# Moving small start-up DMAs from SyncE to GpSimd, and widening the dummy matmuls of the start, in a three-layer CIN kernel

## The chip, the cores and the metric

The kernel runs on one core of a Trainium2 chip. A core has five engines that run their own instruction streams and meet at semaphores: TensorE (PE in the profile; its weight loads are PEld), VectorE (DVE), ScalarE (ACT), GpSimd (POOL) and SyncE (SP). SP, ACT and POOL can issue DMAs. The metric is the device time of one execution in microseconds, as the median of several runs: 736.74 us before the change (three runs, 736.66 to 737.49).

## The reference

A batch of 1024 samples has 39 fields with an embedding of 64 each. Three layers of a compressed interaction network (CIN) follow, all in float32:

```python
def _cin_layer(Xk, X0, W, b):
    O = W.shape[0]
    Hk, Fdim = (Xk.shape[1], X0.shape[1])
    Wr = W.reshape(O, Hk, Fdim)
    return jnp.einsum('bhe,bfe,ohf->boe', Xk, X0, Wr) + b[None, :, None]
X0 = sparse_embedding
Xk = X0
outs = []
for W, b in ((W0, b0), (W1, b1), (W2, b2)):
    Xk = _cin_layer(Xk, X0, W, b)
    outs.append(Xk.sum(axis=-1))
cin_output = jnp.concatenate(outs, axis=-1)
return cin_output @ fc_w.T + fc_b
```

Every layer has 64 outputs. Only sums over the embedding reach the result, one number per sample, through a final linear layer. The biases b0, b1, b2 and fc_b are vectors of 64 words (fc_b: one word).

## The kernel before, in words

The two later layers are folded into the weights first: from W2 and the final weights the kernel makes a small matrix V2 (`v2`, 64 x 40), from W1 and V2 the products `pt` and `pv` (L431), and together with W0, transposed into `pw` (L452), these fill one table `both` of 128 x (39 x 40). What is left for the samples is a sum over pairs of fields, products of two rows of x. Weights for the pairs are taken from `both` into `pairs` (L480 and L482), turned by TensorE (`tr`, L499) and copied to `wa` (L500 and L501).

The samples are done in 32 blocks of 2048 columns (32 samples times 64). For each block GpSimd gathers five tiles of 128 rows, each row one field's values, from a table `xd` in DRAM (`roll`, through L170); every second block it also gathers two smaller tiles `u` and `v` (`roll_small`). VectorE multiplies two gathered tiles into a product `p` (L210; L212 for u and v), and TensorE multiplies `p` by `wa` into PSUM banks `po` (L515, and L535 and L546 for u and v). Six products per block and one joint product per two blocks follow each other as steps; VectorE works four steps ahead of TensorE (`AHEAD`). When a block is through, `finish` reads its banks with ScalarE (L563) and VectorE (L565, which adds the bias `b0s`) and sums them up (L576).

The table `xd` has three DRAM tiles, each for two blocks: 39 rows of fields and a row of ones for each block. `load(n)` writes a block's fields (L164). Block 0 is treated apart: it is loaded in two halves `xh` (L244), gathered straight from there, and copied into `xd` by SP afterwards (L387).

The order of the work on each engine is the order of the program text (a manual schedule); a semaphore is waited for where a buffer is written or read by another engine or a DMA. DMAs of a kind share eight semaphore lanes in turn, so a DMA also waits until the one that used its lane before has landed. In the start-up the queues hold, in order:

- SP: `fcrow`, the first half `xh`, three DMAs of `ones` into `xd` (L253), two for `w0s` (L255), two for `bias` (L357: b1 and b2), two for `b0s` (L359), one for `fcb` (L360), the two copies `xd<-xh` (L387).
- ACT: `w2s`, two halves of `w1s`, the second half `xh`.
- POOL: small set-up work (its last memset is L355), four gathers from the first half `xh`, `load(1)`, four from the second half, tile 4 of block 0, u and v, the five gathers of block 1, `load(2)`, `load(3)`, and then the gathers of block 2.

TensorE's own start is filled with dummy matmuls on constants into a bank `idle` (`spin`, L273). A dummy has 256 columns unless another width is given; each matmul in float32 stands in the profile as two records. There are two at the very start, then after the small matmuls of `fcrow` one of 256 and one of 128, again one of 256 and one of 128 after the four matmuls of `pv` (L397), three behind V2, and one more ahead of the first L515.

Of the kernel before, what the change touches and what calls it, by code (L numbers as in the profile page):

```python
# [60 lines left out]
B, F, E, H = 1024, 39, 64, 64  # L61
FH = F * H
FT = F + 1
# [12 lines left out]
MM = 512  # L76
# [7 lines left out]
NTAB = 3  # L84
# [59 lines left out]
def cin_kernel(ctx: ExitStack, tc: tile.TileContext, x, w0t, b0, w1, b1, w2, b2, fc_w, fc_b, out):  # L144
    nc = tc.nc
# [10 lines left out]
    xd = [dram.tile([2 * FT, BLK], F32, name=f"xd{k}") for k in range(NTAB)]  # L156
# [5 lines left out]
    def load(n, engine=nc.sync):  # L162
        first = n % 2 * FT
        engine.dma_start(  # L164
            xd[n // 2 % NTAB][first : first + F].rearrange("f (b e) -> f b e", e=E),
            xv[:, n * BB : (n + 1) * BB, :],
        )

    def gather_rows(dst, table, k):
        nc.gpsimd.indirect_dma_start(  # L170
            dst, None, table, bass.IndirectOffsetOnAxis(ap=lists[:, k : k + 1], axis=0)
        )

    def roll(n, tiles=range(NT)):
        for i in tiles:
            k = n % 2 * NT + i
            gather_rows(rt[n % 2][:, i], xd[n // 2 % NTAB][: FT if k < NT else 2 * FT], k)

    def roll_small(n):
        table = xd[n // 2 % NTAB].rearrange("f (t c) -> (f t) c", c=SUB)  # L180
        for k, dst in enumerate((ut, vt)):
            gather_rows(dst[n // 2 % 2], table, 2 * NT + k)
# [5 lines left out]
    bias = const.tile([H, 2], F32, name="bias")  # L188
    b0s = const.tile([128, 1], F32, name="b0s")
    fc0s = const.tile([128, 1], F32, name="fc0s")  # L190
    fcb = const.tile([1, 1], F32, name="fcb")
# [24 lines left out]
    with prep as prep:  # L216
# [6 lines left out]
        ones = prep.tile([16, 2, 128], F32, name="ones")  # L223
# [25 lines left out]
        for s in range(2):  # L249
            half = slice(s * FH // 2, (s + 1) * FH // 2)  # L250
            nc.scalar.dma_start(w1s[:, half], w1[:, half])
        for k in range(NTAB):
            nc.sync.dma_start(xd[k][F::FT].rearrange("r (p c) -> p r c", c=128), ones)  # L253
        for s, n in enumerate((NW, F - NW)):
            nc.sync.dma_start(  # L255
                w0s[H * s : H * s + F, 0 : n * H], w0v[:, s * NW * H : (s * NW + n) * H]
# [14 lines left out]
        def spin(n=1, cols=MM // 2):  # L271
            for _ in range(n):
                nc.tensor.matmul(  # L273
                    idle[:, 0:cols],
                    nc.const_aps.tensor(1.0, (128, 128), F32),
                    nc.const_aps.tensor(1.0, (128, cols), F32),
                    start=True,
                    stop=True,
                )

        spin(2)

        tmp = prep.tile([128, 16], F32, name="tmp")
        wide = prep.tile([128, 5, NT], F32, name="wide")
# [3 lines left out]
        def new():  # L288
            used[0] += 1
            return tmp[:, used[0] - 1 : used[0]]  # L290
# [24 lines left out]
        for at, k, h in ((1, 0, 0), (2, 1, 0), (3, 2, 0), (4, 0, H)):  # L315
# [4 lines left out]
                start=True,  # L320
                stop=True,
            )
        spin()
        spin(1, MM // 4)

        nc.vector.tensor_copy(row, place)
        step(row, F, 1.0, j)
# [25 lines left out]
        nc.gpsimd.memset(pairs[:, NPAIR:, 0:SQUARE], 0.0)  # L353
        bothv = both.rearrange("p (a b) -> p a b", b=FT)
        nc.gpsimd.memset(bothv[0:H, :, F], 0.0)  # L355
        for k, t in enumerate((b1, b2)):
            nc.sync.dma_start(bias[:, k : k + 1], t.rearrange("(h o) -> h o", o=1))  # L357
        for h in (0, H):
            nc.sync.dma_start(b0s[h : h + H], b0.rearrange("(h o) -> h o", o=1))  # L359
        nc.sync.dma_start(fcb, fc_b.rearrange("(p o) -> p o", o=1))  # L360

        r, most, seat, far = (new() for _ in range(4))
        both_of = prep.tile([128, 2], F32, name="both_of")
# [41 lines left out]
            blocks.rearrange("p f h -> p (f h)").rearrange("p (f h) -> p f h", h=32),  # L405
            pv[:, 0:320].rearrange("p (h f) -> p f h", f=10),
        )
        spin()
        spin(1, MM // 4)
        nc.scalar.copy(v2[:, F:FT], small[0:H, 2:3])  # L410
        for u, f0 in enumerate(quarters):
            for s in range(2):
# [5 lines left out]

        roll_small(0)
        roll(1)  # L420
        load(2, nc.gpsimd)
        load(3, nc.gpsimd)

# [15 lines left out]
        def copy_t(q):  # L439
            for t in range(2):  # L440
                a = 2 * NQ * q + t
                m = len(range(a, min(F, 2 * NQ * (q + 1)), 2))
                copies[t](  # L443
                    bothv[H:128, a : a + 2 * m - 1 : 2],
                    pt[q][H * t : H * t + H, 0 : m * FT].rearrange("h (a b) -> h a b", b=FT),
                )
# [17 lines left out]
                copies[k](bothv[0:H, a + t : a + t + 2 * m - 1 : 2, 0:F], src[:, :, 0:F])  # L464
        copy_t(2)
        copy_t(3)
        spin(3)
        first = [prods.tile([128, BLK], F32, name="p", tag="p") for _ in range(4)]


# [140 lines left out]
    p = {}  # L611
# [25 lines left out]
    for at, (n, c) in enumerate(steps[:-TAIL]):  # L637
# [26 lines left out]
        if at + AHEAD < len(steps):  # L664
            n, c = steps[at + AHEAD]
# [70 lines left out]
```

## Time and profile before

| what | us |
|---|---|
| median of the runs | 736.74 |
| the profiled execution's own time | 743.94 |
| its span, first to last instruction | 742.2 |
| PE busy | 731.6 (99%) |
| DVE busy | 637.7 (86%) |
| POOL busy | 378.7 (51%) |
| ACT busy | 165.4 (22%) |
| L515, main products on PE | 666.9, 1536 records |
| L210, products on DVE | 434.2, 198 instructions |
| L170, gathers of `r` from `xd` on POOL | 306.4, 156 instructions |
| dummies, L273 | 9.1, 20 records |

The profile is one execution; times in its views count from the start of its span. A busy row says how long an engine had an instruction in work, not that it worked at its best; matmuls are pipelined and their ends are modelled. In the timelines, a bracket behind a row tells how long the engine had been idle before it and what released it; "issue" means that nothing in the profile explains the wait. Rows of SPq are DMAs being issued: their lengths are the time to issue, not to land. A row of POOL with a DMA is the time in which GpSimd makes its descriptors.

### The profile page before, as it was taken

To read this page: it belongs to the slowest core of one execution; us is meant where nothing else is said; L and a number is where in the kernel's file an instruction comes from. 1 tells how busy PE (TensorE), PEld (TensorE's weight loads), DVE (VectorE), ACT (ScalarE), POOL (GpSimd) and SP (SyncE) were. 2 spreads that over 40 slices of the span, in tenths; PEclk is the share of its full clock that TensorE was granted. 3 is DMA by queue.
4 is the path that set the end of the run, shared out by engine and by line. 5 is a ranking of instruction groups with operands and counts; after the bars stand their busy time and mean duration, and the time that the engine had idled before them with its cause. 6 is when DMAs were issued, how large, how long until landed. Compare 5 with 4: busy or idle time off the path is not lost.

```text
span 742.2 us, 6521 instructions
## 1 busy us (share of the span) xinstructions
PE 731.6 (99%) x2460; PEld 322.0 (43%) x2460; DVE 637.7 (86%) x518; ACT 165.4 (22%) x241; POOL 378.7 (51%) x248
## 2 busy tenths in 40 slices
PE   8799999999999999999999999999999999999998
PEld 6344444444444444444444444444444444444443
DVE  4798898888998888898888989888898888899885
ACT  2222122221222212122221222212122221212222
POOL 5867453755444575454656545475553557545300
PEclk9999999999999999999999999999999999999999
DMA  8989777867578785767967677786858866666700
GB/s 244 416 262 399 269 280 283 331 225 279 229 291 334 267 302 220 287 239 301 352 216 274 256 278 296 283 312 221 288 232 296 341 264 250 219 249 263 283 1 1
DMA packets 63866, 197.25 MB, mean 266 GB/s; under 512 B 37846, under 2 KB 37943, under 8 KB 43866
## 3 DMA queue, kind: packets, MB, share of 16 engines
q0 software_dynamic: 28784, 186.17, 64.7%
q1 hardware_dynamic: 34104, 9.23, 5.4%
q10 hardware_dynamic: 946, 1.44, 0.7%
q8 instruction: 19, 0.31, 0.2%
q14 instruction: 13, 0.11, 0.0%
HBM read 196.76 MB, written 10.60 MB: 279 GB/s over the span
## 4 chain that ended last, share of the span: by engine, by line
PE 98%; DVE 1%; issue 0%; another core or an unknown queue 0%; ACT 0%; POOL 0%
PE po L515 90%; PE po L535 4%; PE po L546 2%; PE idle L273 1%; PE pt L431 1%; PE pv L431 0%; PE pw L452 0%; PE tr L499 0%; PE pv L397 0%; DVE g L565 0%; DVE sums L587 0%; ACT z L563 0%; POOL shifts L308 0%; DVE wide L295 0%
## 5 line engine op out<-in xcount | busy, mean ns | idle before, releaser
L515 PE MATMUL po<-p,wa 128*128 128x512 f32 x1536 | 666.9, 595 | 0.0
L210 DVE TENSOR_TENSOR p<-r 128x2048 f32<-128x2048 f32 (+2 forms) x198 | 434.2, 2224 | 74.6 <-PE po L515 74.6
L170 POOL DMA_INDIRECT r<-xd,lists x156 | 306.4, 1964 | 297.6 <-issue 283.8
L515 PEld LDWEIGHTS po<-p,wa 128*128 128x128 f32 x1536 | 290.8, 191 | 371.3 <-issue 352.6
L563 ACT ACTIVATE z<-po,fc0s 64x512 f32<-64x512 f32 x128 | 87.3, 682 | 382.5 <-PE po L546 219.7
L565 DVE SCALAR_TENSOR_TENSOR g<-po,b0s,z 64x512 f32<-64x512 f32 x128 | 95.9, 749 | 9.3 <-ACT z L563 5.3
L558 ACT COPY g<-r 39x1024 f32<-39x1024 f32 x64 | 66.7, 1043 | 151.9 <-DVE sums L576 124.7
L576 DVE TENSOR_REDUCE sums<-g 103x16 f32<-103x1024 f32 x62 | 75.6, 1220 | 2.1
L535 PE MATMUL po<-p,wa 32*64 32x512 f32 x512 | 31.6, 600 | 0.0
L170 POOL DMA_INDIRECT u<-xd,lists x16 | 28.3, 1771 | 5.2 <-issue 5.2
L170 POOL DMA_INDIRECT v<-xd,lists x16 | 28.4, 1777 | 4.9 <-issue 4.9
L212 DVE TENSOR_TENSOR p<-u,v 128x1024 f32<-128x1024 f32 x16 | 19.5, 1218 | 0.0
L535 PEld LDWEIGHTS po<-p,wa 32*64 32x64 f32 x512 | 9.4, 131 | 20.2 <-issue 20.2
L546 PE MATMUL po<-u,wa 32*64 32x512 f32 x256 | 17.0, 587 | 0.0
L170 POOL DMA_INDIRECT r<-xh,lists x8 | 7.8, 973 | 6.8 <-DVE blocks L404 4.6
L273 PE MATMUL idle<-const-float32-1.0 128*128 128x256 f32 (+1 forms) x20 | 9.1, 610 | 1.0 <-PEq L723 0.8
L546 PEld LDWEIGHTS po<-u,wa 32*64 32x64 f32 x256 | 5.8, 132 | 8.0 <-issue 8.0
L443 DVE COPY both<-pt 64x200 f32<-64x200 f32 x3 | 1.1, 358 | 7.7 <-remote 5.2
L273 PEld LDWEIGHTS idle<-const-float32-1.0 128*128 128x128 f32 x20 | 6.0, 324 | 2.8 <-issue 1.8
L499 PE MATMUL tr<-unit,pairs 128*128 128x128 f32 x8 | 2.6, 320 | 4.4 <-remote 3.9
L482 DVE TENSOR_TENSOR pairs<-both 128x2 f32<-128x2 f32 (+27 forms) x59 | 6.0, 171 | 0.4 <-ACT both L443 0.4
L500 ACT COPY wa<-tr 128x128 f32<-128x128 f32 x8 | 2.1, 265 | 16.9 <-PE tr L499 15.9
(88 smaller groups left out, 55.4 us busy)
## 6 DMA issues: line engine op xcount, KB each, us to landing
xd<-in_x SPq DMA_DIRECT2D x26, 312.0 KB
r<-xd,lists POOLq DMA_INDIRECT x156
xd<-in_x POOLq DMA_DIRECT2D x5, 312.0 KB
w2s<-in_w ACTq DMA_DIRECT2D x1, 624.0 KB
w1s<-in_w ACTq DMA_DIRECT2D x2, 312.0 KB
xd<-xh SPq DMA_DIRECT2D x2, 156.0 KB
u<-xd,lists POOLq DMA_INDIRECT x16
v<-xd,lists POOLq DMA_INDIRECT x16
```

The lines of the kernel that those rows point to most:

```text
L170: nc.gpsimd.indirect_dma_start(dst, None, table, bass.IndirectOffsetOnAxis(ap=lists[:, k : k + 1], axis=0))
L210: nc.vector.tensor_tensor(p[:, cols], r[:, i, cols], r[:, k, cols], ALU.mult)
L212: nc.vector.tensor_tensor(p[:, 0:SUB], ut[n // 2 % 2], vt[n // 2 % 2], ALU.mult)
L273: nc.tensor.matmul(idle[:, 0:cols], nc.const_aps.tensor(1.0, (128, 128), F32), nc.const_aps.tensor(1.0, (128, cols), F32), start=True, sto ...
L431: nc.tensor.matmul(pt[q][H * t : H * t + H, g * FT : g * FT + FT], w1v[:, a], v2, start=True, stop=True,)
L515: nc.tensor.matmul(po[n][m], wa[:, c, side : side + 2 * H], p[:, bass.ts(m, MM)], start=n % 2 == 0 and c == 0, stop=n % 2 == 1 and c == NP ...
L535: nc.tensor.matmul(dst[half * H : half * H + H], wa[rows, NPAIR, at : at + H], p[rows, bass.ts(side, MM)], start=t >= 2, stop=t < 2 and ha ...
L546: nc.tensor.matmul(dst[half : half + H], wa[rows, NPAIR + 1, H : 2 * H], ut[n // 2 % 2][rows, bass.ts(side, MM)], start=False, stop=t < 2,)
L558: nc.scalar.copy(gt[H : H + F], rt[n % 2][0:F, 0, bass.ts(m, SUB)])
L563: nc.scalar.activation(z[one], po[n][m][other], AF.Identity, bias=fc0s[other])
L565: return lambda: nc.vector.scalar_tensor_tensor(g[n][m // 2][0:H, at], po[n][m][one], b0s[one], z[one], ALU.add, ALU.mult)
L576: nc.vector.tensor_reduce(sums[:, b_at : b_at + SB], g[n][m // 2].rearrange("p (b e) -> p b e", e=E), AX.X, ALU.add,)
```

## The change

The three DMAs of `ones` go from SP to POOL, where they stand ahead of the first gather. The five DMAs of the biases (`bias` twice, `b0s` twice, `fcb`) go from SP to POOL behind the gathers of block 1 and ahead of `load(2)` and `load(3)`. The first two dummies of 256 columns become one of 512; the two places with 256 and 128 columns get one of 512 each; the three of 256 behind V2 become one of 512 and one of 256. The dummy ahead of the first L515 stays. Lines behind the change move up by one to seven.

```diff
-        for k in range(NTAB):
-            nc.sync.dma_start(xd[k][F::FT].rearrange("r (p c) -> p r c", c=128), ones)
         for s, n in enumerate((NW, F - NW)):
             nc.sync.dma_start(
                 w0s[H * s : H * s + F, 0 : n * H], w0v[:, s * NW * H : (s * NW + n) * H]
...
-        spin(2)
+        spin(1, MM)
...
-        spin()
-        spin(1, MM // 4)
+        spin(1, MM)
...
         bothv = both.rearrange("p (a b) -> p a b", b=FT)
         nc.gpsimd.memset(bothv[0:H, :, F], 0.0)
-        for k, t in enumerate((b1, b2)):
-            nc.sync.dma_start(bias[:, k : k + 1], t.rearrange("(h o) -> h o", o=1))
-        for h in (0, H):
-            nc.sync.dma_start(b0s[h : h + H], b0.rearrange("(h o) -> h o", o=1))
-        nc.sync.dma_start(fcb, fc_b.rearrange("(p o) -> p o", o=1))
+        for k in range(NTAB):
+            nc.gpsimd.dma_start(xd[k][F::FT].rearrange("r (p c) -> p r c", c=128), ones)
...
-        spin()
-        spin(1, MM // 4)
+        spin(1, MM)
         nc.scalar.copy(v2[:, F:FT], small[0:H, 2:3])
...
         roll_small(0)
         roll(1)
+        for k, t in enumerate((b1, b2)):
+            nc.gpsimd.dma_start(bias[:, k : k + 1], t.rearrange("(h o) -> h o", o=1))
+        for h in (0, H):
+            nc.gpsimd.dma_start(b0s[h : h + H], b0.rearrange("(h o) -> h o", o=1))
+        nc.gpsimd.dma_start(fcb, fc_b.rearrange("(p o) -> p o", o=1))
         load(2, nc.gpsimd)
         load(3, nc.gpsimd)
...
         copy_t(3)
-        spin(3)
+        spin(1, MM)
+        spin()
```

## The prediction

> **What bounds the kernel.** I read the page first. Its chain that ended last says almost the whole span is TensorE:
>
> ```profile
> PE 98%; DVE 1%; issue 0%; another core or an unknown queue 0%; ACT 0%; POOL 0%
> ```
>
> L515, the main products, is 90% of it and runs with no gap from about 33 us to the end. The change touches nothing behind block 2, so it can act only through the moment at which L515 starts, the pace of its first matmuls, or a starved block soon after. So the second view is the same chain in order of time, for the first 60 us:
>
> ```profile
> 5.96 1.28 PE pv L397 x8
> 7.24 1.58 PE idle L273 x4
> ...
> 8.92 2.63 PE pt L431 x40
> ...
> 18.50 2.72 PE idle L273 x6
> 21.21 3.12 another core or an unknown queue
> ...
> 25.12 0.45 PE tr L499
> ```
>
> (Start, length, what.) L431 is the V2 stage: W1 times V2 into `pt` and `pv`, with W0's transposes (L452) between. It begins at 8.92, when ScalarE has copied `v2`; the first transpose for the main loop runs at 25.12. The chain ends V2 at 18.26 and then has 3 us of nobody. The third view, VectorE's timeline, shows what really paces it:
>
> ```profile
> 11.09 0.36 DVE L443 COPY both<-pt 64x200 f32<-64x200 f32 x1 [2.51 <-PE pt L431]
> 14.12 0.36 DVE L443 COPY both<-pt 64x200 f32<-64x200 f32 x1 [2.68 <-remote]
> 17.06 1.14 DVE L464 COPY both<-pw 64x390 f32<-64x390 f32 x2 [2.58 <-PE pt L431]
> 20.71 0.36 DVE L443 COPY both<-pt 64x200 f32<-64x200 f32 x1 [2.52 <-remote]
> 23.61 0.36 DVE L443 COPY both<-pv 64x200 f32<-64x200 f32 x1 [2.54 <-remote]
> ```
>
> Each copy takes 0.36 us and waits 2.5 us for a TensorE group (10 matmuls, 10, 20 transposes, 10, 9): about 3 us a group. Matmul ends in a profile are modelled, so I trust the copies: V2 takes 8.92 to 23.61, 14.7 us, and the small matmuls are slow, not the copies. The fourth view, TensorE's timeline at the start of L515:
>
> ```profile
> 28.13 3.19 PE L515 MATMUL po<-p,wa 128*128 128x512 f32 x4
> 31.27 1.88 PE L515 MATMUL po<-p,wa 128*128 128x512 f32 x4
> 33.10 8.75 PE L515 MATMUL po<-p,wa 128*128 128x512 f32 x20
> ```
>
> A record takes 0.80 us, then 0.47, then 0.44. The page's PEclk row shows full clock throughout; the pace contradicts it. TensorE runs at about half rate until about 31 us, V2 included.
>
> **What the Trainium skill says.** "TensorE: Matmul & The Clock Gate", Part 1, says the array idles at half clock and is released after about 3.4 us of sustained work in a free-running window, and falls back after a window of idleness. The 0.80 and 0.44 us agree. Same page, "LDWEIGHTS": a weight load costs by its columns, so V2, one load of 64 columns per 40 streamed, leaves the array poorly used; 14.7 us of it did not bring the clock up, which fits. "DMA: Bandwidth & Descriptors", "Issuing engines are not separate DMA queues", says moving a DMA to another engine saves only issue time. That is what the SP view must be read for.
>
> **The change, part by part.** SP's timeline:
>
> ```profile
> 1.86 4.26 SPq L253 DMA_DIRECT2D xd<-ones  x3
> 6.17 1.33 SPq L255 DMA_DIRECT2D w0s<-in_w0t  x2
> 7.54 1.73 SPq L357 DMA_DIRECT2D bias<-in_b  x2
> 9.43 1.12 SPq L359 DMA_DIRECT2D b0s<-in_b  x2
> ...
> 11.08 1.66 SPq L387 DMA_DIRECT2D xd<-xh  x2
> ```
>
> *Ones off SP*: `w0s` is issued 4.3 us sooner, at 1.86. The transposes that need it are recorded from 11.49, straight behind V2's first half, and by the copies' pace are not executed before 14.1. So I take 0 now. The cover is V2's slowness: were V2 twice as fast, TensorE would want `w0s` at about 11.5, and an old landing near 11 would begin to bind.
>
> *Biases off SP*: the copies `xd<-xh` are issued when `xh` lands instead of at 11.08, up to 1.7 us sooner. They gate the gather of tile 4 (POOL, 19.95, 0.94 us idle where the usual gap is 0.30): 0.64 us sooner at most. Tile 4 is wanted first by the fifth product, near 37 us. 0.
>
> *Ones onto POOL*: three DMAs between its last memset (ends 3.39) and its first gather (8.03). A plain DMA there is 1.05 us (L164), so 3.2 to 4.1 us with gaps: POOL is free at 6.6 to 7.5. 0; if each took 2 us the gathers would slip 1.4 us, and the first product, at 24.89, long behind its data, covers that.
>
> *Biases onto POOL*, behind the last gather of block 1 and ahead of load(2) and load(3):
>
> ```profile
> 31.47 6.36 POOL L170 DMA_INDIRECT r<-xd,lists  x1 [0.30 <-issue]
> 37.82 2.06 POOL L164 DMA_DIRECT2D xd<-in_x  x2
> 45.58 4.36 POOL L170 DMA_INDIRECT r<-xd,lists  x1 [5.70 <-ACT pairs L488]
> ```
>
> No row shows a single-word DMA on POOL. Below: five at 0.93 plus 0.30, 6.2 us. Above: as slow as a gather beside a VectorE product, 2.3 plus 0.3, 13 us. "SBUF — State Buffer", "SBUF: two separate sides", says GpSimd and some VectorE operations exclude each other on one port, so the upper end stays open; I take 7. load(2) is then issued at 44.8 instead of 37.8; with 4.7 us for both loads, their landing and POOL's start, block 2's first gather begins at 49.5 instead of 45.58, 4 us late (10 at the upper end). The lane that load(2) reuses now has to wait for a block 1 gather, which has landed by its turn. Slack: the second tile of block 2 landed near 58.3 and its product on VectorE starts near 65.1 (third of three L210 in a row, 60.66 plus two times 2.2), 6.8 us later; TensorE wants that product only at about 74.5 (L596, which stands ahead of the last three products of block 1, runs at 63.9; three times 3.43 follow), and the product takes 2.3: 7.1 us more. 0 at both ends. Waiting for the moved words: `b0s` (VectorE, 55.2), `bias` (TensorE, 63.9). Issued by 44 to 51 they are there; otherwise the last products of block 1 would queue behind L565. 0.
>
> *Dummies*: 512 columns are two records of 0.84 us at half clock (18.50, 2.72 for six of 256: 0.42 each), 1.68 us; 256 plus 128 were 1.26. First and last groups keep their sums (512; 768). The second ends at about 5.7, before `pv` (5.94): 0. The third grows by 0.42 and ends at about 8.95 instead of 8.53, V2 started at 8.92: 0.05 to 0.1 us lost. Gained: TensorE is busy nearly without a break from 3.99 to 8.95, with 0.24 us missing. The best 3.4 us window is filled 93% (before, 81% in the best position; 65% where it stood in this profile, if windows are counted back in 3.41 us steps from the change of pace at 30.8).
>
> Sum without a clock release: +0.1 of dummies, 0 of the rest. The profiled run took 743.94 with a span of 742.2; the median is 736.74. I apply differences to the median: **736.8**, own range 735.5 to 738.0 since the window's position alone moves half-rate L515 by up to 1.7 us.
>
> **The rivals.** *Clock released at V2.* The 93% window reaches the threshold. For it: dense L515 from 28.13 brought release within 3.4 us. Against it: the threshold is shown only to lie above the 65% of 23.9 to 27.3 us and below the nearly full window behind it; 14.7 us of V2 never reached it, so one window of V2 may drop the clock again. One released window saves 3.4 us of V2: 733.3. Bounds: 1.4 us, if it falls mostly on the dummies, 735.3; all of V2 halved (7.3) and six slow L515 records (2.4), 727.0.
>
> *W0 in front of W1 (slower).* The 380 KB of `w0s` (195.0 and 185.2) now stand right behind `xh` in SP's queue while the second half of `w1s` is landing. At 207 GB/s, the rate of 6.87 to 10.28 us, all of it ahead costs 1.8 us; V2 starts at 10.7: 738.6. It decides once the landing passes 8.7 us, the end of the `v2` copy, by more than 1.5. Against it: bytes interleave, and most of `w1s` is in before `xh` is through, so 0.3 is likelier.
>
> *Single words starve block 2 (slower).* The cover of 13.9 us is gone at 3.1 us per DMA, and 1.5 us are lost at 3.4; at 4 us each, 18.6 us late, 4.7 of stall: 741.4. Against it: the longest row that could bear on a DMA of so few bytes is 2.3.
>
> *No visible effect* is the forecast itself: transfers hidden anyway, the clock as late as before.
>
> **How the numbers follow.** A measurement here can tell 0.2%, 1.5 us: below 735.3 is faster, above 738.2 slower. Chances: clock released 0.37 (threshold between 65% and 97%, 93% filled in about half of the positions, below 80% in a third; and three runs of before within 0.9 us say that 81% does not do it), no effect 0.44, W0 ahead 0.11, starved block 2 and other effects of the new order 0.08. Range 731.5 to 739.0: it leaves out the larger clock gains (0.08) and the worst delays (0.08). Faster 0.37, same 0.44, slower 0.19.
>
> **What would show it.** Right: V2's first record near 9.0, copies on `both` about 3 us apart, the first L515 at 0.8 us a record near 26, block 2's L210 without a DMA wait. Clock rival: copies 1.5 us apart and L515 starting near 22. W0 rival: a gap on TensorE ahead of L431 above 1 us. Block 2: TensorE idle near 74 us, behind an L210 that waits for a gather. I am wrong if V2 is not slow by the clock, or if the unprofiled start differs from this trace: the 7.2 us between the profiled run and the median are not explained by anything above.

## The result, and the profile after

| | before | after |
|---|---|---|
| median of the runs (12 each, taken together) | 736.88 | 738.08 |
| lowest to highest | 735.55 to 739.59 | 736.39 to 739.94 |
| the profiled execution's own time | 743.94 | 736.39 |
| its span | 742.2 | 734.6 |
| V2's first matmul starts | 8.92 | 9.97 |
| first main product on TensorE starts | 26.21 | 20.11 |
| POOL's first gather | 8.03 | 9.44 |
| POOL's first gather of block 2 | 45.58 | 51.75 |

The ratio of the times, after to before, is 1.0011, with a 95% interval of 0.9997 to 1.0025: no change that the measurement can tell, and if there is one, a small loss. Executions of one and the same kernel spread over 4 us, so the two profiles must not be subtracted: the changed kernel's is 7.6 us shorter, though its median is not lower at all.

VectorE's timeline of the changed kernel, its copies out of the V2 stage (start, length; in brackets the idle time before and what ended it):

```profile
11.44 0.36 DVE L441 COPY both<-pt 64x200 f32<-64x200 f32 x1 [2.85 <-PE pt L429]
12.66 0.36 DVE L441 COPY both<-pt 64x200 f32<-64x200 f32 x1 [0.85 <-PE pt L429]
...
16.43 0.36 DVE L441 COPY both<-pv 64x200 f32<-64x200 f32 x1 [0.84 <-PE pv L429]
```

They stand 1.2 us apart, not 3. V2 takes 6.5 us here, from 9.97 to 16.43, where the profile of before showed 14.7. TensorE's timeline of the changed kernel at V2's start and at the start of the main products:

```profile
9.97 2.63 PE L429 MATMUL pt<-v,w1s 64*64 64x40 f32 x40 [0.68 <-DMA w1s<-in_w]
...
20.11 1.10 PE L514 MATMUL po<-p,wa 128*128 128x512 f32 x2
...
21.16 1.88 PE L514 MATMUL po<-p,wa 128*128 128x512 f32 x4
```

Two readings. V2 waits 0.68 us for `w1s`, a wait that the profile of before did not have. And TensorE is on its main products 6 us earlier than there, already at 0.47 us a record. The queues, first SP's timeline and then POOL's, both of the changed kernel:

```profile
1.85 1.25 SPq L253 DMA_DIRECT2D w0s<-in_w0t  x2
8.67 3.22 SPq L381 DMA_DIRECT2D xd<-xh  x2
```

```profile
3.30 1.81 POOL L354 DMA_DIRECT2D xd<-ones  x3
...
25.00 6.36 POOL L170 DMA_INDIRECT r<-xd,lists  x1 [0.31 <-issue]
...
41.82 1.17 POOL L415 DMA_DIRECT2D bias<-in_b  x2
42.94 1.10 POOL L417 DMA_DIRECT2D b0s<-in_b  x2
43.95 0.63 POOL L418 DMA_DIRECT2D fcb<-in_fc_b  x1
...
51.75 1.04 POOL L170 DMA_INDIRECT r<-xd,lists  x1 [4.71 <-DVE g L564]
```

The moved DMAs are cheap on POOL: three of `ones` in 1.81 us, and the five of the biases, which move 64 single words each (`fcb`: one), in 2.8 us (41.82 to 44.58). One gather, at 25.00, takes 6.36 us where its neighbours take about 1 to 2.7; this row becomes important below. The chain that ended last has changed too. The page's line of it, and then two pieces of the chain in order of time:

```profile
PE 88%; DMA 5%; POOL 3%; DVE 2%; issue 1%; ACTq 0%; ACT 0%; DVEq 0%; POOLq 0%; SPq 0%
```

```profile
42.94 7.34 DMA b0s<-in_b
...
50.43 0.69 DVE g L564
```

Before, 98% of the chain was TensorE. Here the chain of the first 68 us runs through the gathers and the transfer of `b0s`, and TensorE only takes over behind them. The `b0s` words land 7.34 us after POOL has issued them, just as VectorE ends the product ahead of L564 (45.94 plus 4.49 is 50.43), so VectorE shows no idle time there; but of the time that the prediction saw between these words and their use, 0.15 us is left.

### The profile page after: what moved, and what is told of

It is laid out like the page before. It is cut to its first block, busy times and chain, and to the rows that moved or that the text cites. A ratio compares the mean times of both kernels' runs of the same rounds, so it can differ in the third digit from the quotient of the medians.

```text
span 734.6 us, 6507 instructions
## 1 busy us (share of the span) xinstructions
PE 729.6 (99%) x2452; PEld 317.5 (43%) x2452; DVE 637.5 (87%) x518; ACT 165.5 (23%) x241; POOL 397.4 (54%) x256
## 4 chain that ended last, share of the span: by engine, by line
PE 88%; DMA 5%; POOL 3%; DVE 2%; issue 1%; ACTq 0%; ACT 0%; DVEq 0%; POOLq 0%; SPq 0%
PE po L514 83%; PE po L534 4%; POOL r L170 3%; PE po L545 2%; DMA r<-xd,lists 2%; DMA xh<-in_x 1%; DMA b0s<-in_b 1%; DMA xd<-xh 1%; DVE p L210 1%; DVE g L564 1%; DVE sums L575 0%; POOL v L170 0%; ACTq L251 0%; POOL bias L415 0%; POOL u L170 0%
## 5 line engine op out<-in xcount | busy, mean ns | idle before, releaser
L170 POOL DMA_INDIRECT r<-xd,lists x156 | 311.2, 1995 | 271.4 <-issue 266.1
L564 DVE SCALAR_TENSOR_TENSOR g<-po,b0s,z 64x512 f32<-64x512 f32 x128 | 95.9, 749 | 9.3 <-ACT z L562 5.3
L170 POOL DMA_INDIRECT u<-xd,lists x16 | 36.8, 2302 | 4.9 <-issue 4.9
L271 PE MATMUL idle<-const-float32-1.0 128*128 128x512 f32 (+1 forms) x12 | 10.2, 970 | 0.8 <-PEq L722 0.8
L164 POOL DMA_DIRECT2D xd<-in_x x5 | 5.2, 1044 | 0.5 <-DMA r<-xd,lists 0.5
L429 PEld LDWEIGHTS pt<-v,w1s 64*64 64x64 f32 x60 | 3.8, 213 | 2.3 <-issue 2.2
L429 PE MATMUL pt<-v,w1s 64*64 64x40 f32 x60 | 4.1, 319 | 0.7 <-DMA w1s<-in_w 0.7
```

The source lines that it names most:

```text
L170: nc.gpsimd.indirect_dma_start(dst, None, table, bass.IndirectOffsetOnAxis(ap=lists[:, k : k + 1], axis=0))
L271: nc.tensor.matmul(idle[:, 0:cols], nc.const_aps.tensor(1.0, (128, 128), F32), nc.const_aps.tensor(1.0, (128, cols), F32), start=True, sto ...
L429: nc.tensor.matmul(pt[q][H * t : H * t + H, g * FT : g * FT + FT], w1v[:, a], v2, start=True, stop=True,)
L564: return lambda: nc.vector.scalar_tensor_tensor(g[n][m // 2][0:H, at], po[n][m][one], b0s[one], z[one], ALU.add, ALU.mult)
```

## The experiments

Every run is set against runs of the kernel before made beside it on the same chip. A range behind a ratio is its 95% interval.

### The kernel before again, and each part alone

The first question was whether the profile that the prediction used is like other executions of the same kernel. No edit:

> The kernel before, unchanged, profiled once more. In its first profile V2 took 14.7 us (copies on both about 3 us apart), in the profile of the changed kernel 6.5 us (copies 1.2 us apart) although its matmuls were recorded at the same pace. Theory A (the long V2 belongs to that one execution): copies 1.2 us apart, V2 from about 8.9 to 15.5, first L515 near 19 to 20, span 733 to 736. Theory B (V2 is slow by the clock or by the order of this kernel, and the change mends it): copies 3 us apart again, first L515 near 26, span near 742. The time is that of the kernel before in both, ratio 1.000.

Measured: 736.14 us against 736.06, ratio 1.0001 (0.9985 to 1.0017). This second profile of the kernel before has a span of 734.6 us. VectorE's copies out of V2, and TensorE's timeline:

```profile
11.26 0.36 DVE L443 COPY both<-pt 64x200 f32<-64x200 f32 x1 [2.09 <-PE pt L431]
12.47 0.36 DVE L443 COPY both<-pt 64x200 f32<-64x200 f32 x1 [0.85 <-PE pt L431]
```

```profile
9.76 2.68 PE L431 MATMUL pt<-v,w1s 64*64 64x40 f32 x40 [0.33 <-DMA w1s<-in_w]
12.37 1.29 PE L452 MATMUL pw<-unit,w0s 39*128 39x39 f32 x20
...
19.93 1.10 PE L515 MATMUL po<-p,wa 128*128 128x512 f32 x2
```

The copies are 1.2 us apart, the last starts at 16.25, so V2 takes 6.5 us, and the first main product starts at 19.93. So the V2 of 14.7 us was a trait of the profiled execution, and the step of the prediction that made it the cover of everything else doesn't hold for the median.

The dummies alone:

```diff
-        spin(2)
+        spin(1, MM)
...
-        spin()
-        spin(1, MM // 4)
+        spin(1, MM)
...
-        spin(3)
+        spin(1, MM)
+        spin()
```

(The middle one at both places.)

> The kernel before with the dummies of the change alone. Theory A (V2 is not paced by the clock, the DMAs carry the change): ratio 0.9995 to 1.0005, V2's first record at 8.9 to 9.0, first L515 within 1 us of the kernel before in the same state. Theory B (dummies release the clock at V2): ratio 0.995 to 0.998 and copies on both closer than 1.2 us; together with the DMAs' part of the change it would come back to the measured 1.0011.

Measured: 735.79 us, ratio 0.9998 (0.9984 to 1.0011): nothing. The busy time by stretches of this kernel (engines' busy time and, in the third column from the right, the granted clock) shows why, for 9.5 to 12.5 and for 13 to 16 us:

```profile
9.50:12.50 3.00, 3.00 (x60) 2.94 (x58) 0.72 (x2) 0.53 (x2) 2.39 (x4) 1.00 0.93 227
13.00:16.00 3.00, 3.00 (x36) 2.52 (x34) 1.55 (x5) 1.28 (x5) 2.39 (x3) 0.50 0.96 292
```

The clock was released for the first half of V2 and fell back to half in the second. TensorE's timeline of the same stretch:

```profile
9.22 2.63 PE L429 MATMUL pt<-v,w1s 64*64 64x40 f32 x40
11.79 0.81 PE L450 MATMUL pw<-unit,w0s 39*128 39x39 f32 x20
```

V2's first 40 records took 2.63 us at full clock. In the profile of the kernel before above, whose trace records no release ahead of 20.08 us, they took 2.68: these matmuls of 64 x 40 don't go by the clock. Only the 20 records of W0's transposes got faster, 0.81 instead of 1.29 us. A released window was worth 0.5 us in V2, not 3.4. Nor does it take wide dummies: in the kernel with the ones alone, next, the trace's record of the clock shows a release from 8.72 to 12.13 us.

The ones alone:

```diff
-        for k in range(NTAB):
-            nc.sync.dma_start(xd[k][F::FT].rearrange("r (p c) -> p r c", c=128), ones)
...
         nc.gpsimd.memset(bothv[0:H, :, F], 0.0)
+        for k in range(NTAB):
+            nc.gpsimd.dma_start(xd[k][F::FT].rearrange("r (p c) -> p r c", c=128), ones)
```

> The kernel before with the three DMAs of ones moved to GpSimd alone, so that w0s is issued at 1.9 us right behind xh. W0-ahead theory: the second half of w1s lands near 9.8 instead of 8.6, xh near 8.6 instead of 7.2, V2 starts near 10 and the first gather near 9.4; ratio 1.001 to 1.002 (0.7 to 1.5 us). Rival (the change's small loss comes from the biases): V2 starts later all the same, but the time is covered by waits behind it, ratio 0.9995 to 1.0005.

Measured: 737.93 us, ratio 1.0022 (1.0010 to 1.0034), a small loss, clear of the noise and just above what the theory of W0 ahead had named. Its TensorE timeline:

```profile
10.40 2.62 PE L431 MATMUL pt<-v,w1s 64*64 64x40 f32 x40 [1.95 <-DMA w1s<-in_w]
```

V2 waits 1.95 us for `w1s`, now that `w0s` is issued at 1.86 instead of near 6. Later TensorE runs dry twice, 0.76 us ahead of its row at 47.18 and 1.16 us ahead of the one at 62.87, each time for a product of VectorE. The second profile of the kernel before has one such spell, 0.67 us ahead of 60.13.

The biases alone:

```diff
-        for k, t in enumerate((b1, b2)):
-            nc.sync.dma_start(bias[:, k : k + 1], t.rearrange("(h o) -> h o", o=1))
-        for h in (0, H):
-            nc.sync.dma_start(b0s[h : h + H], b0.rearrange("(h o) -> h o", o=1))
-        nc.sync.dma_start(fcb, fc_b.rearrange("(p o) -> p o", o=1))
...
         roll_small(0)
         roll(1)
+        for k, t in enumerate((b1, b2)):
+            nc.gpsimd.dma_start(bias[:, k : k + 1], t.rearrange("(h o) -> h o", o=1))
+        for h in (0, H):
+            nc.gpsimd.dma_start(b0s[h : h + H], b0.rearrange("(h o) -> h o", o=1))
+        nc.gpsimd.dma_start(fcb, fc_b.rearrange("(p o) -> p o", o=1))
```

> The kernel before with the five bias DMAs moved to GpSimd alone. W0-ahead theory: V2 and the gathers of block 0 as before, ratio 0.9995 to 1.0005; b0s lands at 45 to 50 us instead of 15.6, and L565 may wait for it by 1 to 2 us without TensorE noticing. Biases theory: block 2's gathers wait for load(2) and L565 waits for b0s, TensorE runs dry between 60 and 90 us for 1 to 3 us, ratio 1.001 to 1.004.

Measured: 737.98 us, ratio 1.0021 (1.0010 to 1.0031), again a small loss. TensorE starts its main products early here, at 18.95, and then runs dry. VectorE's, POOL's and TensorE's timelines of this kernel:

```profile
23.02 5.76 DVE L210 TENSOR_TENSOR p<-r 128x1024 f32<-128x1024 f32 x5
...
43.77 2.29 DVE L210 TENSOR_TENSOR p<-r 128x2048 f32<-128x2048 f32 x1 [6.26 <-DMA r<-xd,lists]
```

```profile
23.37 6.36 POOL L170 DMA_INDIRECT u<-xd,lists  x1 [0.30 <-DVE pairs L482]
```

```profile
46.12 10.57 PE L515 MATMUL po<-p,wa 128*128 128x512 f32 x24 [1.30 <-DVE p L210]
```

Read them from the bottom. TensorE was idle for 1.30 us until 46.12, for a product of VectorE. That product began at 43.77 and had waited 6.26 us for a gather of block 1. The gathers of block 1 were late because the u gather ahead of them took 6.36 us, from 23.37 to 29.73: from shortly after VectorE began five products in a row (23.02 to 28.78) until 0.95 us after their end. That last part is as long as a gather takes undisturbed (0.94). The same is seen in 12 of the 14 profiles: one gather begins about 0.35 us behind the start of the five products, takes 6.35 to 6.37 us and ends 0.94 to 0.96 us behind them. From 28 to 32 us the DMA engines moved 106 GB/s, against 406 from 20 to 24.

The Trainium skill has this under "SBUF — State Buffer", "SBUF: two separate sides": a VectorE instruction with two SBUF inputs and a GpSimd instruction that reads SBUF exclude each other, and while GpSimd is kept out it can't write descriptors and the DMA engines starve (the page tells the second part for another mode of VectorE). This trace agrees in its shape. The page gives the end of the block as about 115 ns behind VectorE's; here it is 0.95 us, the gather's own length.

There is another effect. On POOL, behind the five moved DMAs, the loads of blocks 2 and 3 waited 1.93 and 2.63 us for gathers of block 1 (issued at 46.42 and 50.05), where in the kernel before they follow the gathers at once; that fits the semaphore lanes, whose turns the five DMAs have shifted. No engine is shown waiting for the two loads in turn. The ratio is in the range of the biases theory, and a second dry spell, 1.51 us until 62.15, lies in the stretch that it named; the theory of W0 ahead, which had 1.000 here, can't be the whole.

So two theories stood for the next runs. D: transfers, not TensorE, set the end of the start-up. P: TensorE's own start does, and what the dummies win the late W1 gives back.

### The changed kernel again, W0 behind, a recombination, and a late TensorE

> The changed kernel again, for a second profile and a tighter ratio. Theory D (the start is bound by the stream of gathers, and each moved group delays it a little): ratio 1.001 to 1.003, first main product between 19 and 21 us, and TensorE runs dry for 0.5 to 2 us near 45 or 60 us in most executions. Theory P (TensorE's own start decides; what the dummies gain, the late W1 gives back): ratio 1.000 to 1.001, no gap on TensorE behind the first main product.

No edit. Measured: 737.53 us against 736.69, ratio 1.0009 (0.9998 to 1.0021), in line with the first comparison. Taken with it, a loss of about 0.1% is likely, though neither interval shows it alone. The first main product at 20.49 is as expected; but TensorE has no dry spell. By both its marks, ratio and gap, this run came out as theory P had it, and not D. V2 waited 1.42 us for `w1s`.

The changed kernel with W0 on ScalarE's queue, behind the second half of block 0:

```diff
-        for s, n in enumerate((NW, F - NW)):
-            nc.sync.dma_start(
+        load_half(1, nc.scalar)
+        for s, n in enumerate((NW, F - NW)):
+            nc.scalar.dma_start(
                 w0s[H * s : H * s + F, 0 : n * H], w0v[:, s * NW * H : (s * NW + n) * H]
             )
-        load_half(1, nc.scalar)
```

> The changed kernel with the two W0 transfers taken from SyncE's queue and put on ScalarE's behind the second half of block 0, so that nothing new stands beside W1 and the first half. Theory W (W0 in front of W1 delays V2 and the first gather): V2 starts by 9.4 us, the first gather by 9.0 us, and the ratio to the kernel before falls by 0.001 to 0.002 against the changed kernel. If W0's place does nothing: the same ratio as the changed kernel within 0.001, V2 at 9.9 to 10.4 us.

Measured: 737.57 us, ratio 1.0004 (0.9992 to 1.0016). Its TensorE timeline:

```profile
9.47 2.62 PE L429 MATMUL pt<-v,w1s 64*64 64x40 f32 x40 [0.18 <-DMA w1s<-in_w]
```

The wait for `w1s` is 0.18 us. Over all profiles: with `w0s` issued at 1.85 or 1.86 it was 0.68, 1.95, 1.42 and 2.37 us; in the ten where `w0s` is issued at 3.06 or later, from nothing to 0.53, but for one of 1.31. So W0 does get in front of W1, and V2 starts about 1 us later for it (10.36 on average in the four, 9.31 in the ten). In the median it doesn't show: the ratio lies 0.0005 below the changed kernel's, inside both intervals, where 0.001 to 0.002 were expected. The other half of the expectation missed, since the first gather came at 10.38, later than with W0 on SP. The single times show more; they come below.

The kernel before with the ones on GpSimd, W0 as in the last, and the biases on SP behind the two copies of block 0; the dummies as before:

```diff
-        for k in range(NTAB):
-            nc.sync.dma_start(xd[k][F::FT].rearrange("r (p c) -> p r c", c=128), ones)
+        load_half(1, nc.scalar)
...
-            nc.sync.dma_start(
+            nc.scalar.dma_start(
                 w0s[H * s : H * s + F, 0 : n * H], w0v[:, s * NW * H : (s * NW + n) * H]
             )
-        load_half(1, nc.scalar)
...
         nc.gpsimd.memset(bothv[0:H, :, F], 0.0)
...
+        for k in range(NTAB):
+            nc.gpsimd.dma_start(xd[k][F::FT].rearrange("r (p c) -> p r c", c=128), ones)
...
         for k, cols in enumerate(halves):
             nc.sync.dma_start(xd[0][0:F, cols], xh[k])
+        for k, t in enumerate((b1, b2)):
+            nc.sync.dma_start(bias[:, k : k + 1], t.rearrange("(h o) -> h o", o=1))
+        for h in (0, H):
+            nc.sync.dma_start(b0s[h : h + H], b0.rearrange("(h o) -> h o", o=1))
+        nc.sync.dma_start(fcb, fc_b.rearrange("(p o) -> p o", o=1))
```

(The five lines of the biases at their old place, behind the memset, go.)

> The kernel before with the ones on GpSimd ahead of the gathers, W0 on ScalarE behind the second half of block 0, and the biases left on SyncE but behind the two copies of block 0 into its table; dummies as before. Theory D and W: nothing stands in the way of W1, of block 0, of the loads or of the gathers: V2 at 8.8 to 9.2 us, block 2's loads from GpSimd near 41 us without a wait, ratio 0.997 to 0.999. If SyncE's queue and W0 never mattered: 1.000.

Measured: 736.73 us, ratio 1.0002 (0.9988 to 1.0016). No gain, where 0.997 to 0.999 was expected. V2 started at 10.34 in its profile, after waits of 1.29 us for `w2s` and 0.53 for `w1s`, although everything had been cleared out of W1's way. Up to here, no version beats the kernel before.

The kernel before with TensorE held up behind V2:

```diff
         copy_t(3)
         spin(3)
+        spin(2, MM)
```

> The kernel before with two more dummies of 512 columns behind V2, which hold TensorE's first main product up by 1.7 to 3.4 us and touch no transfer. Theory P (TensorE's start sets the end): the time grows by the delay that the profile shows, 1.7 to 3.4 us, ratio 1.0023 to 1.0046. Theory D (transfers set the end of the start): the delay is made up at the next stall on a gather, the gaps near 45 and 60 us close, ratio 1.000 to 1.001; the part of the delay beyond those gaps (0.8 us in the last profile of the kernel before) is still lost.

Measured: 737.14 us, ratio 1.0004 (0.9991 to 1.0017). Its TensorE timeline:

```profile
14.97 5.46 PE L273 MATMUL idle<-const-float32-1.0 128*128 128x256 f32 x10
...
20.90 1.12 PE L516 MATMUL po<-p,wa 128*128 128x512 f32 x2
```

From the first of these dummies to the first main product it takes 5.93 us, against 3.78 (16.15 to 19.93) in the second profile of the kernel before: 2.15 us of delay. By the ratio the time grew by 0.3 us, at most 1.25 by the interval. At least 0.9 us, and more likely most of it, was made up at the median. Theory P, which wanted the whole delay in the time, falls for the median: there TensorE's start has slack. It doesn't fall for every execution, as the single times below show.

### What decides when block 1's data come

Theory G grew out of the traces so far: the end of the start-up is set by which gather is caught under VectorE's five products. To move GpSimd ahead of VectorE, one line of the kernel before was taken off GpSimd:

```diff
             for i in range(4):
                 gather_rows(rt[0][:, i, cols], xh[k], i)
-            if not k:
-                load(1, nc.gpsimd)
         for k, cols in enumerate(halves):
             nc.sync.dma_start(xd[0][0:F, cols], xh[k])
+        load(1)
```

> The kernel before with one line moved: block 1's load goes from GpSimd, where it stands among the first gathers and takes 1.06 us, to SyncE's queue behind the two copies of block 0. Theory G (the start is decided by how many gathers GpSimd has issued when VectorE begins its five products of 1024 columns in a row, since the gather caught under them takes about 6.4 us and the DMA engines run empty; it costs about 2.5 us when it is the u gather that is caught): u is issued 1.4 us sooner and the caught gather is v or the first of block 1, the median falls by 0.5 to 2 us, ratio 0.9975 to 0.9995, and the slow third of the executions, above 737.5 us, gets rare. Theory W (W1, V2 and the first gather's start decide): V2 and the first gather start as in the kernel before, ratio 1.000.

Measured: 743.47 us against 742.28, ratio 1.0006 (0.9981 to 1.0032). That is not what theory G expected, but two things spoiled the question. On this chip the kernel before itself had a median of 742.28 us, and in this profile V2 took 14.4 us (9.31 to 23.73), as in the prediction's profile. And the moved load was issued at 13.16 and still had packets on the way at 28 us, so that the u gather began at 29.51 only; from GpSimd, that load lands within about 8 us.

The TensorE timeline of this kernel is the better view of a slow V2, since its records show the pauses. One group of records, and the pause ahead of it:

```profile
16.49 0.47 PE L430 MATMUL pt<-v,w1s 64*64 64x40 f32 x4 [0.95 <-issue]
```

Four records go at their usual pace, then some 0.95 us, up to 1.66, pass with no wait that the profile knows, and so on. A slow clock doesn't do that: at half clock 40 such records took 2.68 us without a pause. So the prediction's reading of the slow V2, half clock, doesn't fit this execution, which has a slow V2.

The kernel before with three memsets, which hold up GpSimd's later gathers and move nothing:

```diff
                 load(1, nc.gpsimd)
+                for _ in range(3):
+                    nc.gpsimd.memset(hold, 0.0)
```

(`hold` is a tile of 128 x 512 that nothing else uses; the load stays on GpSimd.)

> The kernel before with three memsets of 128 x 512 words put on GpSimd behind block 1's load, which hold its later gathers up by about 1.5 us and move no byte by DMA. Theory G: the gather caught under VectorE's five products is u or even the fifth of block 0 in nearly every execution, ratio 1.002 to 1.004, stalls of TensorE near 45 and 60 us. Theory W: the first gather and V2 are where they were, ratio 1.000 to 1.0005.

Measured: 739.29 us, ratio 0.9968 (0.9953 to 0.9984): faster, on this chip, against both theories. V2 took 8.3 us in its profile, from 9.08 to 17.39, not 14.4, and the first main product came at 21.07, against 26.97 with the moved load. TensorE came back to its usual pace at 14.72, and the memsets start at 14.69. The median, 3 us lower with an interval clear of 1, says that the slow V2 depends on GpSimd's work at that time. It doesn't say by what way: elsewhere the same gathers run beside a V2 of 6.5 us. What slows V2 stays open. What G says of the rest is there: u was caught, until 31.62, and TensorE was dry for 1.58 and 1.22 us.

The changed kernel with the load moved as above:

```diff
-            if not k:
-                load(1, nc.gpsimd)
...
+        load(1)
         roll(0, (4,))
```

> The changed kernel with block 1's load moved to SyncE in the same way. Theory G: the single words and ones cost the changed kernel nothing by themselves, and what it loses is the caught gather: ratio 0.9975 to 0.9995 to the kernel before, at or below the one of the load alone within 0.001. If what it loses is the biases' place ahead of the loads of blocks 2 and 3, which this leaves there: ratio above the one of the load alone by 0.001 to 0.002.

Measured: 743.52 us, ratio 1.0002 (0.9975 to 1.0029). Theory G's range missed again. By the terms of the expectation this puts the ones' and biases' places at nothing beside the load alone (1.0006), but the intervals reach 0.3% either way, and V2 was slow here too, with a wait of 2.37 us for `w1s` ahead of it, so it says little about an ordinary execution.

The memsets once more, on another chip:

> The kernel of the last set with GpSimd's later gathers held up by three memsets, once more, because V2 was slow in nearly every execution of the kernel before in that set and so the question was not put. Theory G, on a chip where V2 takes 6.5 us: block 1's first product on VectorE starts at 44 to 46 us instead of 39 to 42, TensorE runs dry for 1 to 2.2 us about 25 us after its first main product, and the ratio is 1.002 to 1.004. Theory W: ratio 1.000 to 1.0005. If V2 is slow again in the kernel before (median near 742 us), the ratio falls below 1 and the run says only that the slow V2 depends on when GpSimd's gathers run.

Measured: 737.19 us against 736.59, ratio 1.0009 (0.9993 to 1.0025). Theory G had expected 1.002 to 1.004; the interval reaches below 1, so not even the sign is shown. V2 took 6.5 us, block 1's first product started at 42.37 and not at 44 to 46, and TensorE had no dry spell. VectorE's and POOL's timelines of its profile:

```profile
27.85 2.36 DVE L210 TENSOR_TENSOR p<-r 128x1024 f32<-128x1024 f32 x2 [0.79 <-DMA r<-xh,lists]
```

```profile
23.91 3.96 POOL L170 DMA_INDIRECT r<-xd,lists  x1 [0.30 <-issue]
```

GpSimd was so late that VectorE lacked data and paused behind three of its five products (begun at 23.57; the row shows the other two). In that pause the caught gather got through after 3.96 us. The delay brought its own remedy, and a test of G by intervention this was not.

### The profiles side by side

All profiles with a short V2. "Dry" is the idle time of TensorE near 46 us, "GB/s" what the DMA engines moved from 24 to 40 us, "first to last" the time from the start of TensorE's first to the start of its last main product, "own time" that of the profiled execution:

| kernel | first gather to the five products | what is caught, until | block 1's first product on VectorE | first main product | dry | GB/s | first to last | own time |
|---|---|---|---|---|---|---|---|---|
| after, again | 15.61 | v, 31.04 | 41.41 | 20.49 | 0 | 259 | 708.85 | 736.72 |
| recombination | 15.39 | v, 31.09 | 41.82 | 20.49 | 0 | 290 | 708.81 | 736.86 |
| after | 15.22 | first of block 1, 31.36 | 38.72 | 20.11 | 0 | 337 | 708.91 | 736.39 |
| dummies | 15.18 | u, 29.45 | 43.83 | 18.89 | 1.94 | 214 | 712.16 | 738.42 |
| ones | 15.07 | u, 31.08 | 44.84 | 20.51 | 0.76 | 213 | 711.28 | 739.34 |
| late TensorE | 14.83 | u, 29.30 | 42.28 | 20.90 | 0 | 267 | 708.20 | 736.48 |
| before, again | 14.82 | u, 28.08 | 40.82 | 19.93 | 0 | 298 | 709.11 | 736.41 |
| W0 on ScalarE | 13.94 | u, 31.02 | 44.96 | 19.13 | 2.04 | 231 | 712.80 | 739.29 |
| biases | 13.87 | u, 29.73 | 43.77 | 18.95 | 1.30 | 213 | 712.11 | 738.73 |

(The two kernels with memsets are left out, as their gathers are held up: 711.80 and 204 GB/s with u caught until 31.62, 709.45 and 306 GB/s with the gather freed at 27.87.) Where GpSimd leads by 15.22 us or more, u is out as the five products begin. In the rest u is caught, and four of these six have a dry TensorE and 2.4 to 4 us more from the first to the last main product (in "dummies" the clock also fell back for one window behind the dry spell). In the other two, u got away early, without a pause of VectorE that the profile shows, or TensorE began late. A dry spell appears where block 1's first product comes late compared with TensorE's start: in "biases" the gap runs from 44.82, 25.9 us behind the first main product. "Late TensorE" took the product at 45.93, and VectorE had ended it at 44.6.

What separates the profiles without exception is not the name of the caught gather but how much the DMA engines had moved: 259 GB/s or more without a dry spell, 231 or less with one, the two kernels with memsets included. The time follows: 736.39 to 736.86 us without, 738.42 to 739.34 with. So theory D fits the profiles better than the narrower G. This is an order found afterwards, not an intervention: no run changed the DMA rate alone.

One profile stands for 12 to 22 executions, and it need not be a usual one. The times of the single executions tell what the usual ones are (the two marks were chosen after the times were known):

| kernel | executions | below 736.0 us | above 737.5 us |
|---|---|---|---|
| before, beside the first parts | 59 | 29 | 15 |
| dummies | 14 | 9 | 2 |
| ones | 22 | 0 | 13 |
| biases | 22 | 1 | 14 |
| before, beside the next four | 59 | 19 | 19 |
| after, again | 22 | 0 | 11 |
| W0 on ScalarE | 22 | 5 | 11 |
| recombination | 14 | 4 | 4 |
| late TensorE | 14 | 0 | 4 |

Two things are mixed in a median. With `w0s` issued early, in "ones" and "after, again", no execution is below 736.0 us (nor in the 12 of the first comparison); with W0 behind, 5 of 22 are again, while those above 737.5 stay 11. And the late TensorE has none below 736.0 either, with no larger share above 737.5. That fits two limits: in the quickest executions TensorE's start counts, and V2's wait for W1 with it; in the longer ones the gathers decide, and TensorE has slack. No profile shows an execution below 736.39 us, so the first half rests on times alone. It also shows how little a single profile says: the one of "dummies" is of one of its two above 737.5 us, and the two of the changed kernel, both without a dry spell, stand beside 18 of 34 executions above 737.5. So what the caught gather costs a median is not shown, and the profiles don't say what an earlier start of TensorE is worth.

## Why the prediction came out right, and where its steps were wrong

The number holds: 736.8 was predicted in the range of 731.5 to 739.0, with no visible change as the likeliest case, and the ratio is 1.0011 (0.9997 to 1.0025). The working behind it was in good part wrong, so there is luck in it: most terms were put at nothing because a slow V2 would cover them, and in the usual execution V2 isn't slow.

- **V2 is 14.7 us long and slow by the clock**: the step that failed. The second profile of the kernel before has 6.5 us. Where records show a slow V2 (the two kernels with block 1's load on SP), its matmuls pause, they don't stretch; where it isn't slow, they take the same time at half and at full clock. The half clock at the first main products (0.80 us a record) was read rightly. The prediction named both as what would make it wrong, "V2 is not slow by the clock" and "the unprofiled start differs from this trace", and both came true. The 7.2 us between profiled run and median, which it left unexplained, are mostly this: 26.21 less 19.93 is 6.3 us of later start.
- **Ones off SP, w0s sooner: 0**. The mechanism was put among the rivals and is real: V2 waits for W1 by 0.7 to 2.4 us. "At 207 GB/s all of it ahead costs 1.8 us" was the right size, "0.3 is likelier" was not. The median of the changed kernel hardly moves by it, but not because of V2's slowness: at the median TensorE's start has slack, as the late TensorE showed. The quickest executions do seem to pay for it, and the ones alone cost 0.2%, so this 0 isn't confirmed. The sentence of the skill that queues of different engines interleave on the same DMA engines ("DMA: Bandwidth & Descriptors", "Issuing engines are not separate DMA queues") agrees, with 0.68 to 2.37 us beside it; that only issue time is at stake doesn't: issuing earlier put 380 KB in another transfer's way.
- **Biases off SP**: the first copy of block 0 was issued at 8.67 instead of 11.08, the second, by the chain, at 11.10. No wait of tile 4 is seen in either kernel's ordinary profile: 0 holds.
- **Ones onto POOL**: 1.05 us each was too dear. Three took 1.81 us, and the first gather waited for other things: 0 holds.
- **Biases onto POOL**: "I take 7" us, with a lower bound of 6.2, against 2.8 measured. load(2) was issued at 44.49, near the predicted 44.8, by two errors that cancel, since block 1's gathers ended at 41.8 and not at 37.8. The slack of 13.9 us was counted from a TensorE that starts 6 us too late. VectorE's part of it is gone: block 2's first gather began at 51.75, and two products of block 2 waited 0.76 and 2.46 us for gathers, where the prediction had named no such wait as a sign of being right; TensorE's part held, as it didn't run dry. `b0s` landed 0.15 us before it was wanted. The lane of load(2) was said to be free by its turn; the loads waited 0.50 us in this profile and 1.93 and 2.63 with the biases alone. It cost nothing in this profile; alone, the part cost 0.2%, by a way that the profiles don't settle.
- **Dummies**: 0 holds. The clock rival's condition, release within V2, came true in the profile of the dummies alone (not in the first of the changed kernel, whose W0 transposes took 1.29 us). Its price was the error: 0.5 us instead of 3.4, as V2's matmuls don't follow the clock.
- **Single words starve block 2**: not seen in the changed kernel. TensorE had no dry spell in either of its two profiles.

One thing stays open: each of two parts alone costs 0.2%, with intervals clear of 1, and all three together 0.1% with intervals that touch it. The intervals overlap, so it isn't shown that the whole costs less than a part; but the losses don't add up, as 0.4% lies outside both intervals of the changed kernel. Its two profiles stand on the good side of the table and those of the parts on the bad, but its single times are long nearly as often as theirs, so the table doesn't explain it.

## What to carry to other kernels

Before building on a stage of the one profile at hand, set its own time against the median: here they differed by 1%, 7.2 us, and 6.3 of it sat ahead of the first main product, in the stage that the prediction leaned on. In a start-up where several engines race, delay one of them and see whether the time follows, and look at the single times beside the median: an engine can have slack in the longer executions and none in the shortest. And where GpSimd writes the descriptors of gathers, look for the gather that is several times longer than its neighbours, for the VectorE products that stand over it, and for how little the DMA engines move meanwhile.

## What the runs showed of the hardware that was not expected

- A gather's row on GpSimd stretched from 0.94 to 6.36 us under five VectorE products of 128 x 1024 in a row (5.76 us) and ended 0.94 to 0.96 us behind them, in 12 of 14 profiles. In the kernel with the biases alone the DMA engines fell from 406 to 106 GB/s with it. In another profile such a gather got through in a pause of VectorE of 0.79 us; in one it got through after 3.95 us without a pause that the profile shows.
- Matmuls with 64 x 64 weights and 40 columns took the same time at both clocks: 2.63 us for 40 records at full, 2.68 at half. Transposes of 39 rows took 0.81 us for 20 at full and 1.29 at half.
- In six of the 14 profiles the clock was released for 3.4 us near V2 and fell back to half for 6.8 to 17.1 us, with wide dummies (four) and without (two).
- DMAs of 64 single words, and one of a single word, cost GpSimd 0.55 to 0.63 us each to issue; the landing of `b0s`, behind gathers in work, took 7.3 us in the changed kernel and 10.9 with the biases alone.
- On one chip V2 took 14.4 and 13.4 us in the two profiles without memsets, by pauses of about 0.95 us between groups of four records for which the profile names no cause, and the kernel before ran at 742.28 us there, against 736.06 and 736.69 on two others.
